# Four convolution layers on one core: the spline layer's output add, broadcasts and splines in another order

## The chip, the cores and the metric

The kernel runs on one core of one Trainium2 chip. The metric is the device time of one execution in microseconds (us), the median of the runs shown. One further execution was recorded by the hardware profiler. Every duration below comes from that one.

## The reference, cut to what matters

Four residual layers work on x of shape (8, 16, 128, 128) in float32. The change touches only the last one, a 3x3 convolution whose inputs are splines:

```python
x = x + conv(_gn(x))                       # layer 3, _gn: group normalisation
patches = _extract_patches(x, 3, 1, 1)     # the 9 shifted copies, zero padding
bspl = _b_splines(patches, grid)           # 8 cubic basis functions of every value
out = einsum('bjhwn,ijn->bihw', silu(patches), base_w)
out = out + einsum('bjhwns,ijns->bihw', bspl, spl_w)
out = out + bias_weight[None, :, None, None]
```

A basis function depends only on the distance of the value from the basis function's centre, so the kernel makes the 8 functions once for each value and then takes the 9 shifts as matmuls.

## The kernel before

Layers 0 to 2 come first and are not changed. Layer 3 starts some 10,675 us into the span.

**Turns.** Layer 3 works in 32 turns: a turn t is a band of 8 rows (k) of one half of the images (g, 4 of the 8 images). A turn has four sets q = 0 to 3, one for each image of its half, and each set fills 128 partitions with 16 channels times 8 basis functions. For one turn the work is:

- *Copies*, `spread_rows` (L1152, matmul at L1160): TensorE copies 4 rows of x to all 8 basis functions, into four PSUM tiles `far`, one for each q. A turn has two halves h of 4 rows, so `spread(0)` and `spread(1)`. `far` has 6 buffers of one PSUM bank each, used in rotation: a copy waits until the distance that read the buffer six copies earlier is done.
- *Distances*, `near(h, q)` (L1199, at L1105): ScalarE turns `far` into |distance| in the tile v of set q. I write n0q for the first half and n1q for the second.
- *Clip*, `clip(q)`: VectorE takes min(v, 6) (L1110). I write Mq.
- *Terms*, first part of `finish(q)` of the class Splines: ScalarE makes e and p from v (L1105; eq, pq), VectorE combines them (L1118; Pq) and writes the spline rows 2 to 9 of the tile s (L1125, `put`; Sq). A `far`, e, p and v operation covers 512 or 1024 columns.
- GpSimd copies rows 8 and 9 of the band above into rows 0 and 1 of s (L1214).
- *Convolution*, `convolve(t, lo, hi)` (L1264, matmul at L1278): 15 taps n, 12 on the splines and 3 on silu(x); a tap has one matmul for each q, and the four q use four column groups of the array side by side, each recorded as two passes. The sums of one turn are in the PSUM tile `acc3`, which has 2 buffers.
- *Output add*, the function `finish(t)` (L1288, at L1291): VectorE adds the sums, a bias and the residual `o`, and 8 DMAs (L1298) store the result. I write o(t).
- Every second turn ScalarE makes silu of a band (L152, tile sil), and 16 DMAs (L1242) copy it to the tile `four`. The residual is loaded by 8 DMAs a turn (L1257).

There are three sets of s tiles, so the splines of up to two turns beyond the one being convolved can be kept.

**What sets the order.** `in_turn` chains the instructions of TensorE, of VectorE and of ScalarE in layer 3, each in the order in which the Python code issues them; so the order of the calls in `make` is the order on these three engines. GpSimd and the DMA queue SP are not chained: they stand in the order that the scheduler gives them. All DMAs of the loop go through the SP queue.

**The loop.** `make(t, conv, done)` (L1305) makes the splines of turn t beside the convolution of turn conv and the output add of turn done. It is called for turns 0 and 1 alone and then as `make(t + 2, t, t - 1)`. So the splines are two turns ahead of the convolution. Within one call the order is: taps 0 and 1; `spread(0)` and the four n0q; taps 2 to 6; `spread(1)`; n10, M0, n11, M1, terms 0, n12, M2, terms 1; taps 7 to 14; output add of turn done; n13, M3, terms 2, terms 3. A `first_row` (a single extra row, L1175) comes before `spread(0)` in turns 0 and 1.

Of the kernel before, what the change touches and what calls it, by code (L numbers as in the profile page):

```python
# [100 lines left out]
def kernel(  # L101
# [20 lines left out]
    nc = tc.nc  # L122
# [22 lines left out]
    def lut(out_, in_, func, **kw):  # L145
        name = sets.get(func, str(func))
        last = phase["all"]
        if name != phase["name"]:
            phase.update(name=name, first=None, all=[])
            if name == "exp_ln":  # L150
                begin(nc.scalar.preload_act_table_set("natural_log_exp_and_others").ins, last)
        ins = nc.scalar.activation(out_, in_, func, **kw).ins  # L152
        if phase["first"] is None:
            begin(ins, last)
        else:
            tc.add_manual_dep(ins, phase["first"].name, order, reason="table set")
        phase["all"].append(ins)
        return ins
# [51 lines left out]
    def in_turn(engine, ins):  # L210

        if engine in chain:
            tc.add_manual_dep(ins, chain[engine].name, order, reason="in turn")
        chain[engine] = ins
        return ins
# [3 lines left out]
    for n in range(5):  # L219
        t = cpool.tile([BC, BC], F32, name=f"w1_{n}")  # L220
# [13 lines left out]
    with ExitStack() as l0:  # L234
        wp = l0.enter_context(tc.tile_pool(name="w0", bufs=1))
        with tc.tile_pool(name="x0", bufs=2) as xp:
            bn0 = xp.tile([BC, NCH, 6], F32, name="bn0", bufs=1)
            for j in range(8):
                t = xp.tile([BC, HW // 8], F32, name="xj")
# [102 lines left out]
        def work(name):  # L342
            return tmp.tile([128, 2, 512], F32, tag="work", name=name, bufs=11)
# [28 lines left out]
        class Variances:  # L372
# [19 lines left out]
            def finish(self):  # L392
                w, pv = work("r0"), banks[:, 0]
                r0, sq = w[:, 0], w[:, 1]
                lut(r0, pv, AF.Ln, bias=eps_t, scale=-2.0)
                lut(r0, r0, AF.Exp, scale=-0.5)
                nc.scalar.activation(sq, r0, AF.Square)
                nc.vector.scalar_tensor_tensor(pv, pv, -0.5 * EPS, sq, op0=ALU.add, op1=ALU.mult)
                r = act.tile([128, 512], F32, name="rstd", bufs=2)
                nc.vector.scalar_tensor_tensor(r, pv, 1.5, r0, op0=ALU.add, op1=ALU.mult)  # L400
                return r
# [251 lines left out]
        def step(n):  # L653
            return steps.get(n)

        for n in range(-2, NCH + 3):
            if n + 2 < NCH:
                steps[n + 2] = Step(4 * (n + 2))
            done = steps.pop(n - 2, None)
            new, old, then, ahead = step(n), step(n - 1), step(n + 1), step(n + 2)  # L660
# [5 lines left out]
            def put(i, f, *a):  # L666
                between[i].append(lambda: f(*a))
# [202 lines left out]
    with ExitStack() as l2:  # L870
# [172 lines left out]
        for m in range(count + 4):  # L1043
            c, before, then = (couples[i] if 0 <= i < count else None for i in (m, m - 1, m + 1))
# [37 lines left out]
    with ExitStack() as l3:  # L1082
# [24 lines left out]
        def curve(v, width):  # L1107

            v = v[:, :width]
            in_turn("dve3", nc.vector.tensor_scalar_min(v, v, 6.0).ins)  # L1110
            e = tmp.tile([128, 1024], F32, name="e")[:, :width]
            p = tmp.tile([128, 1024], F32, name="p")[:, :width]
            yield
            act(e, v, AF.Square, scale=1.0 / 3.0, bias=minus)
            act(p, v, AF.Prelu, scale=1.0 / 3.0, bias=minus, alpha=-3.0)
            in_turn(
                "dve3",
                nc.vector.scalar_tensor_tensor(  # L1118
                    p, p, 3.0, e, op0=ALU.subtract, op1=ALU.mult
                ).ins,  # L1120
            )
            yield v, p
# [8 lines left out]
        turns = [(k, g) for k in range(H // 8) for g in range(2)]  # L1131
# [14 lines left out]
        def of(t, q):  # L1146
            return tiles[4 * (t % 3) + q]
# [4 lines left out]
        def spread_rows(t, lo, n):  # L1152

            g = turns[t][1]
            out_ = []
            for q in range(NP):
                p = ps.tile([128, 512], F32, name="far", bufs=6)
                in_turn(
                    "pe3",
                    mm(  # L1160
                        p[:, : n * W],
                        copy[32 * q : 32 * q + 32, g],
                        x[32 * q : 32 * q + 32, lo * W : (lo + n) * W],
                        start=True,
                        stop=True,
                    ).ins,
                )
                out_.append(p[:, : n * W])
            return out_

        def distance(v, p, t, q):
            b = 2 * q + turns[t][1]
            act(v, p, AF.Abs, scale=fac[:, 0, b : b + 1], bias=fac[:, 1, b : b + 1])

        def first_row(t):  # L1175
            ps_ = spread_rows(t, 0, 1)
            v = tmp.tile([128, 1024], F32, name="v", bufs=4)
            for q, p in enumerate(ps_):
                distance(v[:, q * W : (q + 1) * W], p, t, q)
            c = curve(v, 512)  # L1180
            next(c)
            v, p = next(c)
            for q in range(NP):
                cols = bass.ts(q, W)
                put(of(t, q)[:, 1, 1 : 1 + W], v[:, cols], p[:, cols])
                nc.gpsimd.tensor_copy(of(t, q)[:, 0, :], edge)
# [77 lines left out]
        def convolve(t, lo, hi):  # L1264

            k, g = turns[t]
            if lo == 0:
                accs[t] = ps.tile([128, 4, W], F32, name="acc3")
            for n in range(lo, hi):
                s, dw = divmod(n, 3)  # L1270
                for q in range(NP):
                    if s < 4:
                        w_, v = wspl[:, s, dw], of(t, q)[:, s : s + 7 : 2, dw : dw + W]
                    else:
                        w_, v = wbase[:, g, dw], sils[k][:, q, :, dw : dw + W]
                    in_turn(
                        "pe3",
                        mm(  # L1278
                            accs[t][32 * q : 32 * q + 32],
                            w_.rearrange("p a f -> p (a f)"),  # L1280
                            v,
                            start=(n == 0),
                            stop=(n == 14),
                            skip_group_check=True,
                        ).ins,
                    )

        def finish(t):  # L1288
            k, g = turns[t]
            o = outs.pop(t)  # L1290
            ins = nc.vector.scalar_tensor_tensor(  # L1291
                o, accs.pop(t), bias3, o, op0=ALU.add, op1=ALU.add
            ).ins
            in_turn("dve3", ins)
            for q in range(NP):
                for p in range(2):
                    lo = 32 * q + 16 * p
                    nc.sync.dma_start(  # L1298
                        out[2 * q + g, :, 8 * k : 8 * k + 8, :].rearrange(
                            "f (i p) w -> f p i w", p=2  # L1300
                        )[:, p],
                        o[lo : lo + 16],
                    )

        def make(t, conv, done):  # L1305

            sp = Splines(t) if t < len(turns) else None
            if conv is not None:
                convolve(conv, 0, 2)
            if sp:  # L1310
                if sp.k == 0:
                    first_row(t)
                sp.spread(0)
                for q in range(NP):
                    sp.near(0, q)
            if conv is not None:
                convolve(conv, 2, 7)
            if sp:
                sp.spread(1)
                sp.near(1, 0)  # L1320
                sp.clip(0)
                sp.near(1, 1)
                sp.clip(1)
                sp.finish(0)
                sp.near(1, 2)
                sp.clip(2)
                sp.finish(1)
            if conv is not None:
                convolve(conv, 7, 15)
            if done is not None:  # L1330
                finish(done)
            if sp:
                sp.near(1, 3)
                sp.clip(3)
                sp.finish(2)
                sp.finish(3)

        silu(0)
        make(0, None, None)
        residual(0)  # L1340
        make(1, None, None)
        for t in range(len(turns)):
            if t + 1 < len(turns):
                residual(t + 1)
            if t % 2 == 0 and t + 2 < len(turns):
                silu(t // 2 + 1)
            make(t + 2, t, t - 1 if t else None)
        finish(len(turns) - 1)


# [71 lines left out]
```

## Time and profile before

| | |
|---|---|
| median of 3 runs | 11350.83 us (11344.36 to 11351.51) |
| the profiled execution | 11347.98 us |
| its span, first to last instruction | 11345.9 us, so 2.1 us lie around it |
| first copy of layer 3 | 10675.34 us |
| first tap of turn 0 | 10702.24 us |
| first tap of turn 2, then every turn until turn 28 | 10744.79 us, then some 20.4 us each |
| first tap of turn 30, the last two turns having no splines beside them | 11313.01 us |
| last output add | 11339.17 us to 11339.92 us |
| TensorE, VectorE, ScalarE busy in a turn from 10928.50 to 10948.90 us | 17.17, 12.75, 14.11 us |

A timeline line has the start in us, the duration, the engine, the line of the code, the operation, the tiles, and in brackets how long the engine was idle before it and what released it. Several instructions of one kind in a row are merged, so that their duration is that of the group. A window line has, after the stretch and its length, the busy time of each engine with the number of instructions, and then PEclk, the share of full speed that TensorE's clock was granted.

### The profile page before, as it was taken

What the parts mean: (1) busy time and instruction counts of PE and PEld (TensorE: products, weight loads), DVE (VectorE), ACT (ScalarE), POOL (GpSimd) and SP (SyncE); (2) the same over time, 40 slices, a digit from 0 to 9 for tenths busy, and PEclk for the clock granted to TensorE, in tenths of its full rate; (3) what the DMA queues carried; (4) which work ended last, traced back from release to release, by engine and by line L of the source; (5) the groups of instructions that cost most, each with busy time, mean ns of one, the idle gap of its engine ahead of it and who ended that gap; (6) DMA issues with size and microseconds to landing.
All of it is one profiled execution on the core that took longest, in us unless ns stands there. A gap on an engine that the chain in (4) does not pass through costs nothing.

```text
span 11345.9 us, 174363 instructions
## 1 busy us (share of the span) xinstructions
PE 8924.7 (79%) x72492; PEld 2115.6 (19%) x72492; DVE 9125.6 (80%) x6935; ACT 8792.4 (77%) x7187; POOL 4870.3 (43%) x2697
## 2 busy tenths in 40 slices
PE   5999999999986777777777777777777777777788
PEld 1222222222222111111111111111111111111122
DVE  3555555555555699999999999999999999999865
ACT  2555555555543699999999999999999999999876
POOL 3556555565542743333333334343343334344300
PEclk8999999999998799999999999999999999999999
DMA  1000000000002300000000000000000000000022
GB/s 48 12 15 15 15 12 13 15 15 14 13 6 67 130 20 7 7 13 7 7 13 7 7 13 7 7 13 7 7 10 10 7 7 13 7 7 7 20 53 50
DMA packets 185552, 203.94 MB, mean 18 GB/s; under 512 B 42936, under 2 KB 151608, under 8 KB 182712
## 3 DMA queue, kind: packets, MB, share of 16 engines
q1 hardware_dynamic: 180264, 190.81, 6.3%
q8 instruction: 570, 9.34, 0.3%
q10 hardware_dynamic: 4496, 1.97, 0.1%
q14 instruction: 222, 1.82, 0.1%
HBM read 107.15 MB, written 60.04 MB: 15 GB/s over the span
## 4 chain that ended last, share of the span: by engine, by line
DVE 44%; PE 31%; ACT 14%; issue 5%; POOL 2%; DMA 1%; SPq 1%; DVEq 0%; ACTq 0%; POOLq 0%
DVE t L959 22%; PE banks L360 17%; DVE u L965 14%; PE pn L927 10%; ACT t L948 8%; DVE y L518 2%; PE acc L1278 2%; POOL y L527 1%; DVE x L538 1%; ACT u L152 1%; PE pd L927 1%; ACT hid L152 1%; SPq L1242 1%; DMA yd<-y 1%; DVE x L630 1%
## 5 line engine op out<-in xcount | busy, mean ns | idle before, releaser
L927 PE MATMUL pn<-f,wa 32*64 32x512 f32 x18432 | 3424.1, 626 | 1706.7 <-DVE u L965 1672.7
L980 POOL TENSOR_TENSOR v<-t,u 128x1024 f32<-128x1024 f32 x1152 | 2738.0, 2377 | 4027.0 <-DVE t L959 3865.8
L965 DVE TENSOR_TENSOR u<-pn,u 128x1024 f32<-128x1024 f32 x2304 | 2715.3, 1220 | 123.6 <-DVE t L959 6.9
L927 PE MATMUL pd<-f,wb 32*64 32x512 f32 x18432 | 2608.4, 628 | 158.4 <-ACT t L948 92.3
L959 DVE SCALAR_TENSOR_TENSOR t<-t,u 128x2048 f32<-128x2048 f32 x1152 | 2631.2, 2284 | 34.4 <-ACT u L152 33.9
L948 ACT ACTIVATE t<-pd 128x1024 f32<-128x1024 f32 x2304 | 2336.7, 1014 | 320.0 <-PE pn L927 312.6
L152 ACT ACTIVATE u<-t 128x2048 f32<-128x2048 f32 x1152 | 2202.5, 1912 | 54.8 <-PE acc L1011 19.1
L152 ACT ACTIVATE u<-u 128x2048 f32<-128x2048 f32 x1152 | 2190.9, 1902 | 0.0
L927 PEld LDWEIGHTS pn<-f,wa 32*64 32x64 f32 x18432 | 752.0, 132 | 3777.2 <-DVE u L965 3243.1
L972 DVE SCALAR_TENSOR_TENSOR u<-t,u 128x1024 f32<-128x1024 f32 x1152 | 1419.1, 1232 | 37.6
L152 ACT ACTIVATE hid<-banks 128x1024 f32<-128x1024 f32 x576 | 571.4, 1023 | 1044.4 <-PE banks L360 1042.6
L1011 PE MATMUL acc<-u,const 128*32 128x512 f32 x9216 | 1263.2, 621 | 1.9 <-DVE u L972 1.9
L527 POOL TENSOR_TENSOR y<-y 128x1536 f32<-128x1536 f32 x256 | 894.6, 3495 | 830.5 <-DVE y L518 830.5
L518 DVE TENSOR_TENSOR y<-banks,vp 128x1536 f32<-128x1536 f32 x384 | 673.2, 1753 | 274.6 <-PE banks L360 271.3
L544 ACT ACTIVATE sq<-x 128x1024 f32<-128x1024 f32 x384 | 397.9, 1054 | 413.4 <-DVE x L538 290.7
L470 POOL TENSOR_TENSOR pd<-q,kp 128x1536 f32<-128x1536 f32 (+1 forms) x256 | 693.4, 2733 | 6.8 <-PE banks L360 6.7
L927 PEld LDWEIGHTS pd<-f,wb 32*64 32x64 f32 x18432 | 515.3, 132 | 753.3 <-ACT t L948 691.0
L360 PE MATMUL banks<-att,const 32*128 32x512 f32 x2304 | 497.4, 668 | 173.9 <-DVE att L509 96.2
L360 PE MATMUL banks<-h,wfc 64*128 64x512 f32 (+1 forms) x3072 | 619.7, 632 | 14.5 <-DVE h L606 14.5
L1011 PE MATMUL acc<-v,const 128*32 128x512 f32 x4608 | 616.8, 606 | 0.2 <-POOL v L980 0.2
L606 DVE TENSOR_TENSOR h<-banks,x 128x1024 f32<-128x1024 f32 x192 | 232.6, 1211 | 435.5 <-ACT hid L152 227.5
L1278 PE MATMUL acc<-s,wspl 128*32 128x512 f32 x3072 | 386.8, 646 | 92.6 <-DVE o L1291 92.6
(177 smaller groups left out, 7501.1 us busy)
## 6 DMA issues: line engine op xcount, KB each, us to landing
f<-yd SPq DMA_DIRECT2D x512, 101.6 KB
yd<-y SPq DMA_DIRECT2D x320, 130.0 KB
xin<-in_x SPq DMA_DIRECT2D x752, 32.0 KB
four<-sil SPq DMA_DIRECT2D x256, 65.0 KB
xj<-in_x SPq DMA_DIRECT2D x8, 1024.0 KB
xl<-in_x SPq DMA_DIRECT2D x32, 256.0 KB
x1d<-xl SPq DMA_DIRECT2D x32, 256.0 KB
x<-x1d SPq DMA_DIRECT2D x8, 1024.0 KB
```

Source lines behind the costliest of these rows:

```text
L152: ins = nc.scalar.activation(out_, in_, func, **kw).ins
L360: in_turn("pe", mm(*args, skip_group_check=True, **kw).ins)
L470: ins = nc.gpsimd.tensor_mul(t[:, :n].rearrange("p n (a b) -> p n a b", a=4), rows(self.q[d][:, k]).unsqueeze(1).to_broadcast([128, n, 4, W]),
L518: ins = nc.vector.tensor_mul(y.rearrange("p n (a b) -> p n a b", a=4), banks[:, 1:4].rearrange("p n (a b) -> p n a b", a=4), windows(v, j, 3),
L527: in_turn("pool", nc.gpsimd.tensor_add(self.y[k], self.y[k], y).ins)
L927: yield mm(p[64 * (u % 2) : 64 * (u % 2) + 64, u // 2], w[lo : lo + 32, q % 2, n].rearrange("p c f -> p (c f)"), fs[g * NP + q][lo : lo + ...
L948: in_turn("act", nc.scalar.activation(self.t[:, ab], self.pd.pop(ab), AF.Abs).ins)
L959: ins = nc.vector.scalar_tensor_tensor(self.t, self.t, 1.0, self.u, op0=ALU.add, op1=ALU.mult).ins
L965: ins = nc.vector.tensor_mul(self.u[:, ab], self.pn.pop(ab), self.u[:, ab]).ins
L972: ins = nc.vector.scalar_tensor_tensor(r, self.t[:, :, 0], 2.0, r, op0=ALU.subtract, op1=ALU.mult).ins
L980: ins = nc.gpsimd.tensor_mul(self.v, self.t[:, :, 1], self.u[:, :, 1]).ins
L1011: ins = mm(accs[k][32 * q : 32 * q + 32], gather[:, int(part == 1), g], (c.u[:, ab, 0], c.u[:, ab, 1], c.v[:, ab])[part], start=first, sto ...
```

## The change

`make` is split. A new function `begin_turn` creates a turn's splines object and issues its first-row work and its `spread(0)`; it is called for the next turn's splines, inside `make`, before taps 9 to 14. `make` now gets splines that are already begun and makes them one turn ahead of the convolution instead of two: `make(sp of t + 1, t, t - 1, t + 2)`. Only one call runs without a convolution instead of two. Inside `make`, `spread(1)` stands after taps 0 and 1, the output add of the turn before stands directly after it and so ahead of all clips and terms, and no output add stands between terms 1 and M3. In turn 0's call, turn 1's first-row work stands between terms 2 and terms 3. In the last turn half of the 8 stores go through ScalarE's DMA queue.

```diff
             for q in range(NP):
+                eng = nc.scalar if t == len(turns) - 1 and q % 2 else nc.sync
                 for p in range(2):
                     lo = 32 * q + 16 * p
-                    nc.sync.dma_start(
+                    eng.dma_start(
...
-        def make(t, conv, done):
-            sp = Splines(t) if t < len(turns) else None
+        def begin_turn(t):
+            if t >= len(turns):
+                return None
+            sp = Splines(t)
+            if sp.k == 0:
+                first_row(t)
+            sp.spread(0)
+            return sp
+
+        def make(sp, conv, done, then):
             if conv is not None:
                 convolve(conv, 0, 2)
             if sp:
-                if sp.k == 0:
-                    first_row(t)
-                sp.spread(0)
                 for q in range(NP):
                     sp.near(0, q)
+                sp.spread(1)
+            if done is not None:
+                finish(done)
             if conv is not None:
-                convolve(conv, 2, 7)
+                convolve(conv, 2, 9)
             if sp:
-                sp.spread(1)
                 sp.near(1, 0)
...
                 sp.finish(1)
-            if conv is not None:
-                convolve(conv, 7, 15)
-            if done is not None:
-                finish(done)
-            if sp:
                 sp.near(1, 3)
                 sp.clip(3)
                 sp.finish(2)
+            behind = begin_turn(then)
+            if conv is not None:
+                convolve(conv, 9, 15)
+            if sp:
                 sp.finish(3)
+            return behind

         silu(0)
-        make(0, None, None)
+        sp = make(begin_turn(0), None, None, 1)
         residual(0)
-        make(1, None, None)
         for t in range(len(turns)):
...
-            make(t + 2, t, t - 1 if t else None)
+            sp = make(sp, t, t - 1 if t else None, t + 2)
         finish(len(turns) - 1)
```

## The prediction

> **What bounds the kernel now.** The change lies in layer 3 alone, the last 670 us; so I read the waits there first, then the timeline of one steady turn, then the granted clock. The waits (waiter, releaser, us, times, longest) name the loop:
>
> ```profile
> DVE v L1110 <- ACT v L1105: 161.9, 31, 5.9
> ACT v L1105 <- PE far L1160: 112.9, 56, 2.9
> PE acc L1278 <- DVE o L1291: 92.6, 29, 3.5
> ACT e L1105 <- DVE v L1110: 48.1, 33, 1.8
> ```
>
> Every engine waits in every turn, so none is the bound: a ring of dependencies is. The timeline of one turn:
>
> ```profile
> 10907.25 0.74 DVE L1291 SCALAR_TENSOR_TENSOR o<-acc,bias,o 128x512 f32<-128x512 f32 x1
> 10908.14 2.90 PE L1278 MATMUL acc<-s,wspl 128*32 128x512 f32 x16 [3.25 <-DVE o L1291]
> 10910.97 1.80 PE L1160 MATMUL far<-x,const 32*128 32x512 f32 x8
> 10912.70 4.51 PE L1278 MATMUL acc<-s,wspl 128*32 128x512 f32 x40
> 10917.15 1.14 PE L1160 MATMUL far<-x,const 32*128 32x512 f32 x8
> 10918.22 4.52 PE L1278 MATMUL acc<-s,wspl 128*32 128x512 f32 x40
> 10918.31 1.45 ACT L1105 ACTIVATE v<-far,fac 128x512 f32<-128x512 f32 x2 [2.72 <-PE far L1160]
> 10919.11 1.36 DVE L1110 TENSOR_SCALAR v<-v 128x1024 f32<-128x1024 f32 x2 [5.59 <-ACT v L1105]
> ...
> 10926.52 1.23 DVE L1125 SCALAR_TENSOR_TENSOR s<-v,p 128x1024 f32<-128x1024 f32 x1
> 10927.66 0.74 DVE L1291 SCALAR_TENSOR_TENSOR o<-acc,bias,o 128x512 f32<-128x512 f32 x1
> 10928.33 0.68 DVE L1110 TENSOR_SCALAR v<-v 128x1024 f32<-128x1024 f32 x1
> 10928.56 2.84 PE L1278 MATMUL acc<-s,wspl 128*32 128x512 f32 x16 [3.25 <-DVE o L1291]
> ...
> 10932.71 1.23 DVE L1125 SCALAR_TENSOR_TENSOR s<-v,p 128x1024 f32<-128x1024 f32 x1
> ```
>
> Taps 0 and 1 (10908.14), copies, taps 2 to 6, copies of the second half, n10 (10918.31), terms 0 and 1, o (10927.66), and the next turn's taps, which need the acc that o reads: 20.42 us. The sums that o adds were complete at 10925.3; o only stands behind S1 on VectorE. The pause has a second price:
>
> ```profile
> 10928.00:10930.00 2.00, 1.45 (x12) 0.59 (x16) 2.00 (x3) 0.96 (x1) 0.00 (x0) 0.86 0.16 36
> 10930.00:10931.00 1.00, 1.00 (x8) 0.00 (x0) 0.90 (x2) 1.00 (x2) 0.00 (x0) 0.50 0.21 43
> 10931.00:10933.00 2.00, 2.00 (x12) 0.52 (x8) 1.90 (x3) 0.23 (x1) 0.00 (x0) 0.54 0.24 52
> 10933.00:10938.00 5.00, 5.00 (x48) 1.49 (x48) 0.94 (x1) 2.78 (x4) 1.18 (x4) 1.00 0.26 53
> ```
>
> PEclk (third number from the right) is 0.50 for some 3.4 us after the pause. That costs half of it, 1.7 us, on the ring.
>
> [...] a pause of 3.25 us, [...] is enough. In layer 2 a pause of 1.5 us every 5.9 us is not:
>
> ```profile
> 10648.00:10649.00 1.00, 0.00 (x0) 0.00 (x0) 0.90 (x2) 1.00 (x2) 0.80 (x1) 1.00 0.00 0
> 10649.00:10650.00 1.00, 0.56 (x16) 0.24 (x16) 1.00 (x2) 1.00 (x1) 1.00 (x1) 1.00 0.00 0
> ```
>
> [...] P beside a row copy takes 1.42 us against 1.22.
>
> ```profile
> 10688.41 0.73 POOL L1214 COPY s<-s 128x260 f32<-128x260 f32 x1 [12.40 <-DVE s L1125]
> 10688.80 1.42 DVE L1118 SCALAR_TENSOR_TENSOR p<-p,e 128x1024 f32<-128x1024 f32 x1
> ```
>
> [...] Here a store takes 3.63 / 8 = 0.455 us of SP.
>
> **The change part by part.** T is a turn's first tap after the pause.
>
> *Output add first.* o(t-1) needs only acc(t-1), complete before T, and on VectorE stands between S3 and M0. M0 can't start before n10 ends, at T + 3.7, so o (0.67) is hidden there. Its acc is next needed a turn later: the wait PE <- o (92.6 us) goes. Were o itself late, M0 and all terms would queue behind it; its residual is loaded more than a turn ahead. What is late next is the splines.
>
> *One turn ahead.* Taps of turn t+1 now need S3 of the splines made beside turn t. The new ring: taps 0 and 1, 16 passes at 0.109 (the last 240 passes took 26.14 us) = 1.74; `spread(1)` to n10, 1.16 (10917.15 to 10918.31); n10 to S3's end: 14.40 (10918.31 to 10932.71), less the 0.67 of o that stood ahead of M3, plus 1.23 = 14.97 (VectorE, and not ScalarE, is late from P1 on, so the 0.67 counts in full); TensorE's wake 0.16 (o's end to 10928.56). Sum 18.03. Behind the waiting tap of q3 stand on TensorE all other taps of the turn and both copies; n10 on ScalarE and through it all terms wait for them, which is why the whole pause counts.
>
> *Row copies.* GpSimd now gets each copy's source ready by S of the same turn, so three of four fall beside the next M and P. In the start-up turn that moved the next S by 0.11, 0.11 and 0.07: 0.3. It could be 0 or, with both operations held up, 0.8. Turn: 18.3.
>
> *spread(0) half a turn ahead.* It needs the `far` buffers of n11 (done at T + 4.3) and comes at T + 9; n00 can't start before T + 15. Hidden by over 5 us. The next n00 to n02 run beside P3 and S3, n03 after S3, done by T' + 0.6 (T' + 1.3 after a silu of 1.4); n10 is due at T' + 2.9. Hidden.
>
> *TensorE.* 120 passes 13.1 + two copies of 1.07 = 15.2. Taps 0 of q0 to q2 need only S0 to S2, so they run ahead of the pause: S2 ends at T + 15.6, q2's tap ends near 16.6, the pause is 1.7[...]. I allow a drop of 1.7 us in one of ten turns: 5 us in all. Bounds: none (0) to every turn (53).
>
> *Queues.* SP issues 16 silu copies (10.25), 16 residual loads (10.2) and 16 stores (7.3) in two turns: 27.7, about 30 with a landing wait, of 36.6. The loads stand behind the stores but are due over a turn later: nothing. GpSimd's two copies behind the sil memset wait for a DMA but are due two turns later: nothing.
>
> *Start.* Terms 3 of turn 0 now follow turn 1's first row. From the start-up timeline: P2 and S2 end at 10694.7, first-row M, e and p until 10696.4, e3 and p3 until 10698.6, P3 and S3 until 10701.2: first tap at 10701.3 instead of 10702.24. The clock is at half there in both programs: taps, copies and n10 take 5.7 (10702.24 to 10707.95) instead of 2.9, so turn 1 starts at 10701.3 + 18.3 + 2.8 = 10722.4.
>
> *End.* 30 turns of 18.3, less 2.0 for the last two of 7 rows (19.4 and 19.2 instead of 20.4): turn 31's taps start at 10722.4 + 549 - 2 = 11269.4. They take 13.1, wake 0.1, o 0.75: 11283.3. Before, 8 stores and landing took 11339.92 to 11345.9 = 6.0; with 4 on each queue 4 x 0.455 less: 4.2. End 11287.5, with the clock allowance 11292.5: 53.4 less than the span of 11345.9. The profiled execution would be 11347.98 - 53.4 = 11294.6; the median lies 2.85 above that execution: 11297.5.
>
> **The rivals.**
> *The clock falls in every turn.* [...] Against: layer 2. It gives 53 instead of 5: 11345.
> *Slower: half speed all the way from T to n10.* [...] Then 2.9 us a turn are lost: 31 x 2.9 - 5 = 85 more, 11382. It decides from a loss of 58.4 / 31 = 1.9 us a turn. [...]
> *Less contention.* No row copy costs anything and no drop: 31 x 0.3 + 5 = 14 less, 11283; TensorE's own 15.2 is no bound then.
> *It doesn't do what it says.* If o kept waiting in VectorE, 20.4 a turn stay and only start and end gain: 31 x 2.1 = 65 back, 11362. Nothing speaks for that: acc is complete before T.
>
> **How the numbers follow.** Forecast with its near neighbours, to 11320: 0.66. Under 11276 (a ring shorter than measured): 0.07. Clock in most turns, 11320 to 11350: 0.19. Not doing what it says, 11350 to 11370: 0.01. Slower[...]: 0.07. A measurement here tells 0.2%, 23 us, from no change, so faster means under 11328: 0.66 + 0.07 + a third of 0.20 = 0.80; same 0.13; slower 0.07. The range from 11276 reaches to 11338, into the clock case, and leaves out 0.07 + 0.13.
>
> **What would show it.** The wait PE <- o vanishes and PE acc <- DVE s takes its place with about 1.7 us in each of 31 turns; turns of 18.3; PEclk 1.00 over most turns; row copies beside P; ScalarE's n10 still waiting for `far`. A PEclk of 0.9 in every turn, or first taps waiting for GpSimd or a DMA, would make it wrong.

## The result, and the profile after

The changed kernel takes 11288.35 us (median of 6 runs, 11287.3 to 11293.7) against 11349.4 us before (median of 6 runs): a ratio of 0.9948, 95% interval 0.9935 to 0.9961 (the two medians alone give 0.9946). The prediction was 11297.5 us. The profiled execution took 11288.42 us with a span of 11286.6 us.

Layer 3 began at 10673.42 us in it and at 10675.34 us before. In all the profiled executions below it began between 10663.9 and 10677.6 us, though nothing ahead of it differs. So I compare the **length of layer 3**, from its first copy to the span's end (670.56 us before, 613.18 us after), and the mean distance of two output adds ("a turn": 20.36 us before, 18.46 us after, taken from the 5th to the 27th add everywhere).

The waits of layer 3 in the changed kernel (waiter, releaser, us, times, longest):

```profile
ACT v L1105 <- PE far L1160: 66.6, 31, 3.1
PE acc L1278 <- DVE s L1125: 48.2, 32, 4.4
```

The wait of TensorE for the output add (92.6 us) is gone; a wait for the splines, half as long, has its place. Waits that are put down to a DMA come to 0.9 us in all, at three weight loads. One turn in the timeline:

```profile
10902.90 0.74 DVE L1291 SCALAR_TENSOR_TENSOR o<-acc,bias,o 128x512 f32<-128x512 f32 x1
10903.13 1.88 PE L1278 MATMUL acc<-s,wspl 128*32 128x512 f32 x10 [1.46 <-DVE s L1125]
10904.94 1.14 PE L1160 MATMUL far<-x,const 32*128 32x512 f32 x8
10906.10 1.45 ACT L1105 ACTIVATE v<-far,fac 128x512 f32<-128x512 f32 x2 [2.22 <-PE far L1160]
...
10912.54 0.73 POOL L1214 COPY s<-s 128x260 f32<-128x260 f32 x1 [9.03 <-DVE s L1125]
10912.93 1.42 DVE L1118 SCALAR_TENSOR_TENSOR p<-p,e 128x1024 f32<-128x1024 f32 x1
10914.45 1.23 DVE L1125 SCALAR_TENSOR_TENSOR s<-v,p 128x1024 f32<-128x1024 f32 x1
...
10918.45 1.66 PE L1278 MATMUL acc<-s,wspl 128*32 128x512 f32 x6
10920.18 1.23 DVE L1125 SCALAR_TENSOR_TENSOR s<-v,p 128x1024 f32<-128x1024 f32 x1
10921.56 1.88 PE L1278 MATMUL acc<-s,wspl 128*32 128x512 f32 x10 [1.45 <-DVE s L1125]
```

Read it as the ring: T at 10903.13; taps 0 and 1; `spread(1)` at 10904.94; n10 at 10906.10, T + 2.97; the terms, with row copies beside the products P1 and P2 (1.42 instead of 1.22); S3 ends at 10921.41, 15.31 after n10; the next T 0.15 later. The sum is 18.43. The output add lies in a gap of VectorE, which waits for n10 until 10906.91, and nothing waits for it. The six passes at 10918.45 are the taps 0 of q0 to q2, ahead of the pause. The granted clock (third number from the right) stays up over all turns:

```profile
10713.00:11283.00 570.00, 524.51 (x4224) 141.38 (x4216) 398.85 (x398) 439.76 (x496) 93.37 (x152) 1.00 0.26 55
```

And the end, where two queues issue the last stores beside each other; the span ends 4.53 us after the add's end, before 5.98 us:

```profile
11282.10 1.73 SPq L1300 DMA_DIRECT2D out<-o  x4
11282.11 1.81 ACTq L1300 DMA_DIRECT2D out<-o  x4
```

### The profile page after: what moved, and what is told of

Its sections match the earlier page's. It is cut to its first block, busy times and chain, and to the rows that moved or that the text cites. A ratio compares the mean times of both kernels' runs of the same rounds, so it can differ in the third digit from the quotient of the medians.

```text
span 11286.6 us, 174493 instructions
## 1 busy us (share of the span) xinstructions
PE 8919.1 (79%) x72492; PEld 2113.4 (19%) x72492; DVE 9133.7 (81%) x6935; ACT 8790.6 (78%) x7187; POOL 4911.4 (44%) x2697
## 4 chain that ended last, share of the span: by engine, by line
DVE 46%; PE 30%; ACT 14%; issue 5%; POOL 2%; DMA 1%; SPq 1%; DVEq 0%; ACTq 0%; POOLq 0%
DVE t L959 22%; PE banks L360 17%; DVE u L965 14%; PE pn L927 10%; ACT t L948 8%; DVE y L518 2%; DVE p L1118 1%; DVE s L1125 1%; ACT u L152 1%; POOL y L527 1%; DVE x L538 1%; PE pd L927 1%; ACT hid L152 1%; DMA yd<-y 1%; PE acc L1278 1%
```

## The experiments

My theory: a ring through TensorE's first taps sets the turn, first through o and after the change through S3. Its rivals: the chain of ScalarE and VectorE is late by itself; the later copies, not the add, bring the gain; the clock alone makes the difference. Each ratio is to the kernel before, measured beside it on the same chip. The chips differ (medians of the kernel before from 11342.44 to 11349.69 us), so two rows are better compared by their layer 3 than by their medians.

| kernel | median us | ratio (95% interval) | layer 3, us | a turn, us |
|---|---|---|---|---|
| the change | 11288.35 | 0.9948 (0.9935 to 0.9961) | 613.18 | 18.46 |
| add first only | 11218.2 | 0.9889 (0.9876 to 0.9903) | 544.83 | 15.92 |
| two turns ahead | 11229.88 | 0.9898 (0.9885 to 0.9912) | 558.47 | 16.33 |
| row copies left out | 11265.13 | 0.9930 (0.9918 to 0.9943) | 592.00 | 17.69 |
| add at its old place | 11299.04 | 0.9960 (0.9947 to 0.9974) | 626.89 | 18.90 |
| q3 first in tap 0 | 11331.81 | 0.9983 (0.9977 to 0.9990) | 652.32 | 19.84 |
| six v buffers | 11283.66 | 0.9948 (0.9933 to 0.9963) | 614.38 | 18.46 |
| copies ahead of the taps | 11221.92 | 0.9888 (0.9873 to 0.9903) | 545.91 | 16.23 |
| add first, six v | 11216.0 | 0.9881 (0.9867 to 0.9896) | 536.94 | 15.71 |
| add first, six v, silu later | 11204.47 | 0.9873 (0.9858 to 0.9887) | 527.22 | 15.47 |
| the change, with copies ahead, six v, silu later | 11204.94 | 0.9879 (0.9863 to 0.9896) | 530.90 | 15.74 |

### Where the gain comes from: the add alone, in the kernel before

```diff
             if conv is not None:
                 convolve(conv, 0, 2)
+            if done is not None:
+                finish(done)
...
                 convolve(conv, 7, 15)
-            if done is not None:
-                finish(done)
```

> The kernel before with one edit: the output add is issued directly after taps 0 and 1 and so ahead of all clips and terms; copies, the two turns of lead and the tail stay. My theory of the ring: with two turns of lead no tap waits for a term of the last turn, so the pause of TensorE goes, and the ring that is left is n10 to the end of S3 (15.3 us), n03 of the next turn, which waits for S3's v tile, and the copies and n10 behind it: about 16.4 us a turn, some 11234 us. First rival: the chain of ScalarE and VectorE alone sets the 18.4 us of the changed kernel, and lead costs nothing: about 11288 us. Second rival: the later copies are what counts and the place of the add alone brings little: over 11330 us.

11218.2 us: twice the gain of the whole change, from one of its parts. TensorE's timeline has no pause:

```profile
10913.00 1.91 PE L1278 MATMUL acc<-s,wspl 128*32 128x512 f32 x16
...
10928.33 1.91 PE L1278 MATMUL acc<-s,wspl 128*32 128x512 f32 x16
```

No group of this stretch has a wait in brackets; a turn without silu takes 15.33 us (10913.00 to 10928.33), which is TensorE's own work, and one with silu 16.49. I had put 16.4 on a ring through n03, which is not what sets the turn: TensorE itself is the bound, and in every second turn its copies wait 1.2 us for ScalarE. The rivals of the terms' chain and of the later copies both fall.

### The lead of one turn: the changed kernel, two turns ahead

```diff
         residual(0)
+        sp = make(sp, None, None, 2)
...
-            sp = make(sp, t, t - 1 if t else None, t + 2)
+            sp = make(sp, t, t - 1 if t else None, t + 3)
```

> The changed kernel with the splines two turns ahead of the convolution again (one more turn made before the loop), all else as changed. My theory: taps no longer wait for S3 of the splines made beside the last turn, the pause of 1.45 us and the 3 us of taps, copies and n10 behind it leave the ring, and about 16.4 us a turn remain (n10 to S3, then n03 and n10): with one more start-up turn some 11234 us, and TensorE paused by waits on copies or not at all. Rival: the terms' chain sets the turn whatever the lead: 18.4 us a turn, about 11288 to 11298 us. Slower rival: the extra start-up turn costs more than the loop gives: over 11300 us.

A turn takes 16.33 us on average; 16.4 was expected, but the agreement is luck. The ring through n03 would make every turn equal, while here turns of 15.35 and 17.2 us alternate: the short ones are TensorE's own work, as in the experiment above, and the long ones have a silu. What holds is that without the wait for S3 the turn falls. The step from two turns of lead to one costs 613.18 - 558.47 = 54.7 us in this order of issue. The three steps from before to after, in layer 3: the add first gives 125.7; the rest of the change, at two turns of lead, takes back 13.6; one turn of lead takes back 54.7; 57.4 are left. The 13.6 are mostly 0.41 a turn, in TensorE's copies, which wait longer in the turns with silu:

```profile
10909.79 3.02 PE L1160 MATMUL far<-x,const 32*128 32x512 f32 x8
```

Eight passes take 1.14 without a wait, here 3.02, in the kernel above 2.29: `spread(1)`, which now stands ahead of taps 2 to 8, needs the `far` buffers that n00 and n01 read, and these stand behind silu.

### Is the ring what I put? The copies ahead of the taps

```diff
+            if sp:
+                for q in range(NP):
+                    sp.near(0, q)
+                sp.spread(1)
             if conv is not None:
                 convolve(conv, 0, 2)
-            if sp:
-                for q in range(NP):
-                    sp.near(0, q)
-                sp.spread(1)
```

> The changed kernel with spread(1) issued after the four n0q but ahead of taps 0 and 1, all else as changed. If the ring is what I put (T, taps 0 and 1, spread(1), n10 to S3's end), then n10 no longer waits for T: it follows n03 at about T + 0.7 instead of T + 2.97, the turn falls by 2.2 us to 16.2 us, near TensorE's own 15.3, and the kernel takes about 11220 us. Rival: ScalarE or VectorE is late by itself and n10's wait only fills slack: turns of 18.4 us and 11288 us. Slower rival: the copies, waiting for the `far` buffers of n00 and n01 ahead of the taps, hold TensorE up: over 11288 us.

Four lines in another order bring the changed kernel from 613.18 to 545.91 us in layer 3, a turn from 18.46 to 16.23 (expected 16.2). ScalarE's timeline shows how:

```profile
10898.47 4.10 ACT L1105 ACTIVATE v<-far,fac 128x512 f32<-128x512 f32 x6
...
10916.56 2.12 ACT L1105 ACTIVATE v<-far,fac 128x512 f32<-128x512 f32 x3 [1.02 <-PE far L1160]
```

The group of six at 10898.47, in a turn with silu, is the four n0q, n10 and n11 without a gap; the group of three at 10916.56 is n03, n10 and n11 of a turn without: n10 no longer waits for T, taps and copies. No operation became shorter; taps 0 and 1 only left the ring. That shows the ring, and that the terms' chain is not what sets 18.4 us. It is what is left: n03 starts 0.12 after S3's end (10916.44), n10 0.68 later, and the next S3 ends 15.32 after that, a ring of 16.1 us. It also shows that one turn of lead is not dear in itself: in this order it takes less than two turns of lead in the order of the change (558.47). The copies do hold TensorE up for 1.6 us in turns with silu (2.70 instead of 1.14 for a group of eight), but that costs less than the ring gave.

### The clock: q3 first in tap 0

```diff
-                for q in range(NP):
+                for q in (range(NP) if n else (3, 0, 1, 2)):
```

> The changed kernel with tap 0 issued in the order q3, q0, q1, q2 instead of q0 to q3: the same passes, but those of q0 to q2 now stand behind the wait for S3 too, so that TensorE's pause grows from 1.45 us to about 3.1 us in each turn. By my reading of the clock[...], PEclk falls to 0.50 for 3.4 us in most turns; taps, copies and n10 behind the pause take up to 1.5 to 1.7 us longer, turns of about 19.9 us, some 11335 us. Rival: a pause of 3 us doesn't matter to the clock, or the clock not to the ring: PEclk 1.00 or turns of 18.4 us, about 11288 us.

The same work takes 652.32 us in layer 3, 39 us more, from a longer pause alone. The first taps of two turns that follow each other:

```profile
10935.61 2.50 PE L1278 MATMUL acc<-s,wspl 128*32 128x512 f32 x16 [2.96 <-DVE s L1125]
...
10955.61 1.93 PE L1278 MATMUL acc<-s,wspl 128*32 128x512 f32 x16 [2.88 <-DVE s L1125]
```

Sixteen passes take 1.93 us at full speed and 3.54 behind such a pause (at 10776.24). Most turns last 20.14 us, every fifth 18.5: the clock costs **1.65 us a turn**. The prediction said 1.7. In the kernel before, one turn is of this kind, 18.78 us from add to add instead of 20.42; its first taps run at full speed, those of the next turn don't:

```profile
11071.34 1.93 PE L1278 MATMUL acc<-s,wspl 128*32 128x512 f32 x16 [3.24 <-DVE o L1291]
...
11090.11 3.46 PE L1278 MATMUL acc<-s,wspl 128*32 128x512 f32 x16 [3.24 <-DVE o L1291]
```

That answers the third rival, and largely in its favour. By this turn the kernel before takes 18.78 us at full clock, and the changed kernel takes 18.44; with the clock lost it is 20.42 before and 20.14 here. So of the 1.98 us a turn that the change gains, 1.64 is the clock, which the shorter pause keeps up, and only some 0.3 is a shorter ring. The first experiment and the copies ahead of the taps gain their further 2.2 to 2.5 us from the ring alone, since the clock is full in the changed kernel already.

Window lines of this run, with PEclk third from the right:

```profile
10936.80:10940.20 3.40, 3.40 (x20) 0.66 (x16) 0.00 (x0) 0.05 (x1) 0.00 (x0) 0.50 0.39 87
...
10954.00:10971.00 17.00, 15.39 (x136) 4.26 (x136) 11.69 (x13) 12.62 (x15) 2.27 (x4) 1.00 0.21 42
```

The slow stretch, PEclk 0.50, lies from 10936.8 to 10940.2, 1.2 us behind the end of a pause of 2.96 us. The next pause, from 10952.73 to 10955.61, is 2.88 us long, and PEclk stays at 1.00 behind it. In the kernel before, the pauses ahead of 11071.34 and 11090.11 are both 3.24 us long: PEclk is 1.00 behind the first, from 11071 to 11089.85, and 0.50 behind the second, from 11089.85 to 11093.26. So the length of the pause alone doesn't tell the two outcomes apart, and what does is not shown by these lines.

### The add back at its old place in the changed kernel

```diff
                 sp.spread(1)
-            if done is not None:
-                finish(done)
...
                 sp.finish(1)
+            if done is not None:
+                finish(done)
                 sp.near(1, 3)
```

> The changed kernel with the output add back between terms 1 and M3, all else as changed. By my sum the chain n10 to S3 gets 0.67 us longer: 19.1 us a turn and a pause of TensorE of about 2.1 us[...], so that the granted clock falls in at least part of the turns: between 11309 us (no turn) and 11350 us (most turns), likeliest 11320 to 11340. Rival: [...]the clock stays up: 19.1 us a turn, 11309 us, PEclk 1.00. Second rival: the add hides in slack of VectorE at its old place: 18.4 us a turn, 11288 us.

11299.04 us, and the expectation failed in two points. A turn is 18.90 us, 0.46 more and not 0.67; and PEclk is 1.00 from 10740 to 11200 us. The timeline has both reasons:

```profile
10917.27 0.74 DVE L1291 SCALAR_TENSOR_TENSOR o<-acc,bias,o 128x512 f32<-128x512 f32 x1
10917.49 0.40 POOL L1214 COPY s<-s 128x260 f32<-128x260 f32 x1 [2.53 <-DVE s L1125]
...
10918.53 1.22 DVE L1118 SCALAR_TENSOR_TENSOR p<-p,e 128x1024 f32<-128x1024 f32 x1
...
10923.70 1.88 PE L1278 MATMUL acc<-s,wspl 128*32 128x512 f32 x10 [1.45 <-DVE s L1125]
```

The add pushes 0.67 into the chain, but the row copy of q1 now lies beside the add and not beside the next P, which takes 1.22 instead of 1.42: 0.67 - 0.20 = 0.47. And the pause is 1.45 us still. It runs from the end of q2's tap, which always follows S2, to S3: S2 and S3 lie 2.47 us apart (P3 and S3), whatever comes ahead of them. A longer chain makes TensorE wait earlier, in q2's tap (2.12 instead of 1.66 for the six passes). So the pause never came to the 2.1 us of the expectation, and what such a pause does to the clock isn't shown by this run.

### The row copies

```diff
-                if self.k:
+                if self.k == 1:
                     nc.gpsimd.tensor_copy(t[:, 0:2, :], of(self.t - 2, q)[:, 8:10, :])
```

> The changed kernel with GpSimd's two-row copies from the band above made only in turns 2 and 3; every later turn convolves old values in rows 0 and 1, so this part of the computation is left out. If the copies cost the chain what I put (0.3 to 0.4 us a turn, three products P at 1.42 instead of 1.22): P 1.22 everywhere, turns of about 18.0 us, TensorE's pause about 1.1 us, some 11276 us. If they cost nothing on the path: 18.4 us a turn and 11288 us. If TensorE's first taps wait for them in the changed kernel unseen: more than 1 us a turn, under 11255 us.

A turn is 17.69 us, 0.75 less than 18.44, more than I had expected. The terms in the timeline of VectorE:

```profile
10921.85 1.22 DVE L1118 SCALAR_TENSOR_TENSOR p<-p,e 128x1024 f32<-128x1024 f32 x1
10923.10 1.23 DVE L1125 SCALAR_TENSOR_TENSOR s<-v,p 128x1024 f32<-128x1024 f32 x1
```

P takes 1.22 here, and S starts 0.03 us after P's end (10921.85 + 1.22 = 10923.07). In the changed kernel it is 0.10 later (10912.93 + 1.42 = 10914.35; S at 10914.45), and in the kernel before 0.13 (10925.17 + 1.22 = 10926.39; 10926.52). So the chain from n10 to S3's end is 14.64 without copies (10915.09 to 10929.73) and 15.31 with them. The prediction's 14.97, taken from rows of before, contained some 0.33 of such gaps. The copies' other 0.34 is the overlap with P1 and P2 (twice 0.20, less 0.06 in the gaps), against 0.3 predicted; the last 0.1 is between S3's end and T (0.05 instead of 0.15).

The gaps go with the number of engines that S waits for, not with a copy still at work. In the records of all twelve traces, but for two S in each of five of them, S of 1024 columns starts 0.03 us after P where it waits for P alone, 0.10 where it waits for GpSimd's copies too, long done or not, and 0.13 where it waits for TensorE as a third. This run itself has eight S of the second kind, at 0.10. The first tap behind S3 is alike: it starts 0.06 us after S3 in this run's turns without copies, where it waits for VectorE alone, and 0.15 in the changed kernel, where it waits for GpSimd too.

### Is n03 hidden? Six buffers of v in the changed kernel

```diff
-                    self.v[q] = tmp.tile([128, 1024], F32, name="v", bufs=4)
+                    self.v[q] = tmp.tile([128, 1024], F32, name="v", bufs=6)
```

(and so where else v is taken)

> The changed kernel with six buffers of the tile v instead of four, all else as changed. n03 then no longer waits for S3. By my prediction n03 is hidden (it ends at about T + 0.7, and n10 behind it can't start before T + 2.97): turns of 18.4 us and about 11288 us, while ScalarE's wait for S3 (15.9 us in the changed kernel) goes. Rival: n03 stands on the ring of the changed kernel as it does two turns ahead: some 0.6 to 1 us a turn less, 11257 to 11270 us.

A turn stays at 18.46, layer 3 at 614.38; ScalarE's wait for S is gone from the list, and the ratio to the kernel before is the same. n03 was hidden, as predicted.

### A faster version

The first experiment's kernel, with half of the last stores on ScalarE's queue and six v buffers:

> The first experiment's kernel (output add first, nothing else) with six buffers of the tile v instead of four and half of the last turn's stores through ScalarE's queue. There, turns take 15.3 and 16.5 us in turn, the longer ones with a silu ahead of n00. If the buffers of v (n03 waits for S3) cost it: about 0.3 us a turn less, 11206 us. If only the silu ahead of n00 does: turns unchanged, and the tail alone gives 1.8 us: 11216 us.

Its four runs (11202.55 to 11223.25 us) can't be told from the first experiment's. The profile can: layer 3 is 7.9 us shorter, 1.4 of it in the tail (4.6 instead of 6.0 after the last add), the rest 0.21 a turn, since the copies of a turn with silu take 1.89 us instead of 2.29. So the v buffers cost some of the wait and silu the rest. Then also silu behind the n0q:

```diff
                 for q in range(NP):
                     sp.near(0, q)
+            if band is not None:
+                silu(band)
```

> As the kernel with six v buffers, and the silu of every second turn is issued after the four n0q instead of ahead of them. If TensorE's waits of 1.2 us in every second turn come from n00 standing behind silu (its `far` buffers come free late), every turn is TensorE's own 15.3 us: about 11200 us. Rival: silu then delays n10 and so the terms, and the wait only moves: no change from the kernel with six buffers.

```profile
10925.99 1.91 PE L1278 MATMUL acc<-s,wspl 128*32 128x512 f32 x16
...
10941.32 1.91 PE L1278 MATMUL acc<-s,wspl 128*32 128x512 f32 x16
```

Turns of 15.33 us (10925.99 to 10941.32) and 15.56 us: at TensorE's own work but for 0.2 in every second one. With 11204.47 us it is faster than the kernels before and after. The same three edits in the changed kernel:

> The changed kernel with spread(1) ahead of taps 0 and 1, six buffers of v, and silu issued after spread(1) instead of ahead of n00. Without silu ahead of n00 the copies no longer hold TensorE for 1.6 us in every second turn: turns near TensorE's own 15.3 us, 28 of them 0.8 us less than with the earlier copies alone: about 11200 us, layer 3 in some 524 us. Rival: with one turn of lead tap 0 of q3 still waits for S3, and silu ahead of n10 delays S3: 16 us or more in every second turn, about 11215 us.

11204.94 us on another chip: the ratios, 0.9879 and 0.9873, can't be told apart, and layer 3 is 3.7 us longer. It gets there by another way than I expected: turns of 16.06 and 15.34 us, since the first group of taps still waits in the turn that follows one with silu, 8.55 us instead of 7.96:

```profile
10902.28 8.55 PE L1278 MATMUL acc<-s,wspl 128*32 128x512 f32 x72
```

The rival's half is right: with one turn of lead silu, ahead of n10, still delays S3 (its end is at 10902.76, and q3's tap follows at 10902.91) and with it the taps. The shorter start (first add 42.06 us after layer 3's begin, 56.70 with two turns ahead) makes up for most of that.

## Why the prediction was right

| step | predicted | measured |
|---|---|---|
| taps 0 and 1, `spread(1)`, n10 after T | 2.90 | 2.97 |
| n10 to S3's end, row copies in it | 14.97 + 0.3 | 15.31 |
| S3 to T | 0.16 | 0.15 |
| a turn | 18.3 | 18.43 |
| pause of TensorE | 1.7 | 1.45 |
| loss by the clock, all turns | 5 | 0 |
| T of turn 0, from the start of layer 3 | 25.96 | 25.78 |
| turn 0 | 21.1 | 19.71 |
| turn 1's T to turn 31's | 547.0 | 549.31 |
| turn 31's taps and add | 13.95 | 13.85 |
| tail | 4.2 | 4.53 |

From the start of layer 3 the working gives 612.16 us without the clock's allowance; 613.18 were measured. That they lie so close is in part luck: turn 0 was put 1.4 us too long, the turns behind it 2.3 and the tail 0.3 too short. The 9.2 us between 11297.5 and 11288.35 are mostly outside the ring: 5 of clock allowance that wasn't needed; 1.9 by which layer 3 began earlier; 2.9 that I added because the median of before lay that far above its profiled execution, while after the two agree to 0.1; less 1.0 for layer 3 itself, and 0.3 for what lies around the span.

- *Output add first.* One line of before was misread: the sums that o at 10927.66 adds are those of the turn before, whose last taps ran from 10902.13 to 10904.9; at 10925.3 the sums of the turn after them were complete. The part itself is right, since it goes by acc(t-1): the add lies at 10902.90 to 10903.64, M0 starts at 10906.91, the wait is gone. Put back it costs 0.46 a turn.
- *One turn ahead.* Right in each term, to 0.07 us. That the turn is n10's way to S3 and back through T is shown by the copies ahead of the taps, which take 2.2 us out of it.
- *Row copies.* Right in place, and 0.34 for 0.3 in size over the rows of before that the sum was taken from. Leaving the copies out gives 0.75, because those rows held waits for GpSimd already; the sum didn't see them as such. P takes 1.42 us beside a copy (10912.93 in the changed kernel) and 1.22 without copies (10921.85 in the run without them).
- *spread(0), n03, silu.* Hidden, as predicted: six v buffers change nothing, and the turns with and without silu are equal (18.44; one of 18.80, in which an S starts 0.46 after P, has no cause that the trace shows).
- *TensorE and the clock.* The pause was put 0.25 too long: q2's tap ends 1.16 after S2 instead of 1.0, and the next T comes 2.62 after S2 instead of 2.7, a distance that P3 and S3 alone fix. The allowance of a drop in one of ten turns was an estimate, and too cautious: PEclk is 1.00 from 10713 to 11283 us. That the clock stays up is most of the gain: 1.64 of 1.98 us a turn.
- *Queues.* Right: waits for a DMA come to 0.9 us in the whole loop.
- *Start.* The half-speed stretch was expected to last through turn 0's path to n10 (5.7 us for 2.9); the path took 4.46, since the clock was full by 10703 us (PEclk 1.00 from 10703 to 10713). That is 1.2 of the 1.4 us.
- *End.* 0.3 too little in the tail.

Of the rivals, the clock falling in every turn was a matter of the pause: with 2.96 instead of 1.45 us it happens in four turns of five, at 1.65 a turn, where that rival had put 1.7 in every turn. The slower one, half speed all the way from T to n10, which would cost 2.9 us a turn, isn't seen even there: the slow stretch lasts 3.4 us and costs 1.65. The rival with less contention had the wrong sign, since the copies cost what they were put at. The prediction was silent on one thing: its own ring says that 2.97 us of TensorE's work came onto it, with a pause behind, only because the lead was shortened while taps 0 and 1 stand ahead of `spread(1)`. It never asked what the add alone would do. The answer was 68 us better than the change.

## What to carry to other kernels

When an edit cuts a ring of waits, write down the ring that is left and ask which part of the same edit put each term on it: here one part gave 125.7 us and two others took 68.3 back. With each engine held to the order of issue, it matters less how much work there is than what stands behind a wait: copies issued ahead of a waiting tap instead of behind it are worth 2.2 us a turn. And a ring's price has two parts, the waits and the clock: here pauses of some 2.9 us took PEclk to 0.50 for 3.4 us in four turns of five, and pauses of 1.45 us left it at 1.00.

## What was not expected of the hardware

- With q3 first in tap 0, a pause of 2.9 us costs the clock in four turns of five, 1.65 us a turn, and nothing in the fifth; in the changed kernel the pauses of 1.45 us never did in 570 us.
- One engine more to wait for goes with a later start even where that engine was done long before: 0.07 us for VectorE's S (0.10 instead of 0.03 after P), 0.03 for a third (0.13), and 0.09 for TensorE's first tap (0.15 instead of 0.06).
- In the kernel before, PEclk is 0.50 from 10929.43 to 10932.84 and from 11089.85 to 11093.26 us: 3.41 us each time.
- The start of layer 3 moved by up to 14 us between executions of kernels that are alike up to there.
